# Attention probabilities turned by the DMA queue for three query tiles of four, with one ring of buffers for both kinds

## The chip, the cores and the metric

The kernel runs on one core of one Trainium2 chip. The time is device time in microseconds (us) from launch to end. Before the change it is 1529.46 us, the median of three runs (1526.32 to 1533.48).

The engines are named as the profile names them: PE is TensorE (PEld its weight loads), DVE VectorE, ACT ScalarE, POOL GpSimd, SP SyncE, whose queue issues most of the DMAs. Each engine works through its own instructions in order and waits at the first whose semaphores are not there yet.

## The reference, cut to what matters

Four sequences of 1024 tokens with 256 features run through four layers, each added to its input: a linear recurrence, a gated feed-forward layer, attention, and the feed-forward layer again. The change lies in the attention, which is, for each of 8 heads of 64:

```python
scores = jnp.einsum('bqhd,bkhd->bhqk', q, k) * scale      # 1024 x 1024 per head
attn = jax.nn.softmax(scores, axis=-1)
out = jnp.einsum('bhqk,bkhd->bqhd', attn, v)
```

The feed-forward layer that runs beside it picks, per token, the 32 largest of 256 gates (`top_k`) and multiplies with them.

## The kernel before, in words

There are three parts. The first, about 0 to 300 us, is the recurrence. The last, from about 1335 us, is the second feed-forward layer. Between them the attention runs, from about 378 to 1303 us, with the first feed-forward layer's remaining tiles (`f1.tile`, 24 tiles of 128 tokens) and the preparation of later work filled in beside it.

The attention's work is cut into **units**: a batch b (4), a half nb of its queries (2), a pair of heads g (4), and a tile q of 128 queries (4), so 128 units. The generator `heads` (L856) makes them one after another. A unit has two **steps**, one for each head j of the pair, so there are 256 steps. A step is:

- scores: four PE matmuls of 128 queries by 512 keys into `sc` (L886; keys are held in a high and a low part). `sc` has two buffers in PSUM.
- the row's maximum on DVE (L890), from PSUM.
- the exponential on ACT (L894), which also gives the row's sum; the result `pr` has three buffers.
- the transpose of `pr`, since the following product needs keys on the partitions. There are two ways.

The **PE way** (q odd, 64 units): eight PE transposes of 128x128 float32 (L905) into PSUM, and two ACT copies of 128x512 out of it into `p0`/`p1` (L910; in the last batch one of the two is done by DVE, L908).

The **DMA way** (q even, 64 units): the exponential is shifted by 2 to the 11th (one more small DVE instruction, L892), ACT casts `pr` to float16 (L897), POOL subtracts that from `pr` to get the remainder in float16 (L898), both halves stand in `pd` (128x2048, two buffers), and SP issues one DMA transpose of it into `d0` or `d1` (L899; two buffers each).

Then `values_sum` (L920) multiplies the transposed probabilities with the values and divides by the row sums. A unit of the PE way takes 16 float32 matmuls (the profile counts each float32 pass, 32 in all). A unit of the DMA way takes 48 float16 matmuls (high and low probabilities with high values, and high probabilities with low values; L930). Both need: the reciprocal of the row sums on DVE (L924), its spreading to 128 columns `rows` on POOL (L926), a PE transpose of that (L938), an ACT copy `rb` (L940) and a DVE product (L941).

When a unit is summed is set by two lists. A unit of the PE way is put on `pending` and summed in the first step of the next unit. A unit of the DMA way is put on `late` and summed in the second step of the next unit of the DMA way, which is two units later. At the end of each batch both lists are emptied at once (L917).

Around it, `merge` (L963) takes one step of `heads` and then those steps of the side work whose time, counted in steps, has come (L1187 to L1213). What each engine does first is then decided by a scheduler with a model of the instructions' durations; it fixes one order for each engine before the kernel runs.

The side work uses the same engines. For the text that follows these lines matter: the gate tiles' top-k on DVE (L674) in `wk`, with POOL's L613, L628, L656, L658 and L659 and DVE's L636; the output product's split on ACT and POOL (L952, L953); and the layer norms, whose short DVE instructions are L55 to L66.

Of the kernel before, what the change touches and what calls it, by code (L numbers as in the profile page):

```python
# [10 lines left out]
F32 = mybir.dt.float32  # L11
# [3 lines left out]
F16 = mybir.dt.float16  # L15
# [6 lines left out]
P = 128  # L22
B = 4
T = 1024
D = 256
KD = D // P
TPB = T // P
# [4 lines left out]
PAIRS = HEADS // 2  # L32
# [147 lines left out]
class Banks:  # L180


    def __init__(self, pool, bufs):
        self.pool, self.bufs = pool, bufs

    def tile(self, shape, tag, name):
        return self.pool.tile(shape, F32, tag=tag, name=name, bufs=self.bufs[tag])
# [300 lines left out]
class Ffn:  # L488
# [100 lines left out]
    def tile(self, i, sp, psum, tags, out=None, fast=False, parts=None, tt=None, fine=False):  # L589


        nc, w = self.nc, self.w
        pool = nc.vector if fast else nc.gpsimd
        x = self.x[i]
        blk, tk = i // 4, slice((i % 4) * P, (i % 4 + 1) * P)
        full = None
        if blk in self.full:
            full = sp.tile([P, D], F32, tag="full", name="full")
            nc.sync.dma_start(full, self.full[blk][:, i % 4, :])
        pl = psum.tile([P, 2, D], tags[0], "pl")  # L600
        self.logits_product(pl, i)


        nr = TOPK // 8
        m8 = sp.tile([P, 2, nr, 8], F32, tag="m8", name="m8")
        e8 = sp.tile([P, 2, 8], F32, tag="e8", name="e8")
        nm = sp.tile([P, 2], F32, tag="nm", name="nm")
        ssum = sp.tile([P, 2], F32, tag="ssum", name="ssum")
        ex = sp.tile([P, 2, D], F32, tag="ex", name="ex")
        wk = sp.tile([P, 2, D], F32, tag="wk", name="wk")  # L610
        for s in range(2):
            self.ordered(nc.vector.max, m8[:, s, 0, :], pl[:, s, :])
        nc.gpsimd.tensor_scalar(nm, m8[:, :, 0, 0], -1.0, 0.0, ALU.mult, ALU.add)  # L613
        for s in range(2):
            nc.scalar.activation(  # L615
                ex[:, s, :], pl[:, s, :], AF.Exp, bias=nm[:, s : s + 1], accum_out=ssum[:, s : s + 1]
            )
            self.last_exp = nc.scalar.activation(e8[:, s, :], m8[:, s, 0, :], AF.Exp, bias=nm[:, s : s + 1]).ins
        yield
        for r in range(nr):  # L620
            for s in range(2 if r else 0):
                self.ordered(nc.vector.max, m8[:, s, r, :], wk[:, s, :])
            for s in range(2):
                v, k = (wk, m8[:, s, r, :]) if r else (ex, e8[:, s, :])
                self.ordered(nc.vector.match_replace, wk[:, s, :], k, v[:, s, :], 0.0)
            if fine and r < nr - 1:
                yield
        pool.tensor_tensor(ex, ex, wk, ALU.subtract)  # L628
        rs = sp.tile([P, 2], F32, tag="rs", name="rs")
        nc.vector.reciprocal(rs, ssum)  # L630
        yield

        q = i % 4
        norm = self.norm[blk]
        if full is not None:
            nc.vector.scalar_tensor_tensor(full, full, rs[:, 0:1], ex[:, 0, :], ALU.mult, ALU.mult)  # L636
            ob = full
        else:
            if tt is not None:
                pf = psum.tile([P, D], tags[2], "pf")  # L640
                self.full_product(pf, tt, q)
            else:
                xn = sp.tile([P, D], F32, tag="fxn", name="fxn")
                with self.tc.issue_after(self.convolved):
                    nc.scalar.activation(
                        xn, x, AF.Identity, bias=norm[:, 1, q : q + 1], scale=norm[:, 0, q : q + 1]
                    )
                pf = self.product(sp, psum, tags, xn, None, parts)
            ob = sp.tile([P, D], F32, tag="ob", name="ob")
            nc.scalar.mul(ob, pf, rs[:, 0:1])  # L650
            pool.tensor_tensor(ob, ob, ex[:, 0, :], ALU.mult)  # L651
        yield

        xg = sp.tile([P, D], F32, tag="xg", name="xg", bufs=2)
        sc = sp.tile([P, 2], F32, tag="sc", name="sc")
        pool.tensor_scalar(sc, norm[:, :, q], rs[:, 1:2], 0.0, ALU.mult, ALU.add)  # L656
        nc.scalar.activation(xg, x, AF.Identity, bias=sc[:, 1:2], scale=sc[:, 0:1])
        pool.tensor_tensor(xg, xg, ex[:, 1, :], ALU.mult)  # L658
        nc.gpsimd.tensor_tensor(x, x, ob, ALU.add)  # L659
        pi = self.product(sp, psum, tags, xg, w.bias, parts)  # L660
        if out is None or fast:
            nc.vector.tensor_tensor(x, x, pi, ALU.add)
        else:
            yi = sp.tile([P, D], F32, tag="yi", name="yi")
            nc.scalar.copy(yi, pi)
            nc.gpsimd.tensor_tensor(x, x, yi, ALU.add)
        if out is not None:
            nc.sync.dma_start(out[i // 4][:, i % 4, :], x)
        yield
# [103 lines left out]
class Attention:  # L773
    def __init__(self, tc, x, ident, ident64, wqk, wvo, wd, sp, wp):
        self.nc, self.x, self.ident, self.ident64 = tc.nc, x, ident, ident64
        self.wqk, self.wvo, self.wd, self.sp, self.wp = wqk, wvo, wd, sp, wp
        self.hp = None
        self.k, self.xnt, self.qs, self.on = {}, {}, {}, {}

        self.sident = wp.tile([HD, HD], F32R, tag="sident", name="sident")  # L780
# [75 lines left out]
    def heads(self, b, psum):  # L856
# [2 lines left out]

        nc, sp, wp = self.nc, self.sp, self.hp  # L860
        kh, kl, la, lb = self.k[b]
        late, pending = [], []
        for nb, g, q in (
            (nb, g, q)
            for nb in range(2)
            for g in range(PAIRS)
            for q in ((0, 2, 1, 3) if b == B - 1 and nb and g == PAIRS - 1 else range(4))
        ):
            by_dma = q % 2 == 0
            if g == 0:  # L870
                self.on[b, nb, q] = wp.tile([P, PAIRS, P], F32, tag=f"on{q}", name=f"on{q}")
            qs = self.qs[b, nb, g]
            ssum = sp.tile([P, 2], F32, tag="ssum", name="ssum", bufs=4)
            if by_dma:
                pts = [wp.tile([P, 2 * TPB, P], F16, tag=f"d{j}", name=f"d{j}", bufs=2) for j in range(2)]
                parts = ((0, lb[0]), (TPB, lb[0]), (0, lb[1]))
                terms = [(v[:, c, :], i + c) for c in range(TPB) for i, v in parts]
            else:
                pts = [wp.tile([P, TPB, P], F32, tag=f"p{j}", name=f"p{j}") for j in range(2)]
                terms = [(la[:, c, :], c) for c in range(TPB)]  # L880
            for j in range(2):
                sc = psum.tile([P, T], "sc", "sc")
# [10 lines left out]
                pr = wp.tile([P, T], F32, tag="pr", name="pr", bufs=3)  # L893
                nc.scalar.activation(pr, sc, AF.Exp, bias=nm, accum_out=ssum[:, j : j + 1])  # L894
                if by_dma:
                    pd = wp.tile([P, 2, T], F16, tag="pd", name="pd", bufs=2)
                    nc.scalar.copy(pd[:, 0, :], pr)  # L897
                    nc.gpsimd.tensor_tensor(pd[:, 1, :], pr, pd[:, 0, :], ALU.subtract)  # L898
                    nc.sync.dma_start_transpose(pts[j], pd.rearrange("p i k -> p (i k)"))  # L899
                else:  # L900
                    for half in range(2):
                        pt = psum.tile([P, 4, P], "t", "ptp")
                        for kk in range(4):
                            kc = 4 * half + kk
                            nc.tensor.transpose(pt[:, kk, :], pr[:, kc * P : (kc + 1) * P], self.ident)  # L905
                        dst = pts[j][:, 4 * half : 4 * half + 4, :]
                        if half == 0 and b == B - 1:
                            nc.vector.tensor_copy(dst, pt)  # L908
                        else:
                            nc.scalar.copy(dst, pt)  # L910
                if j == 0 and pending:
                    self.values_sum(*pending.pop(0), psum)
                if j == 1 and late and by_dma != (q > 0 and (b, nb, g) == (B - 1, 1, PAIRS - 1)):
                    self.values_sum(*late.pop(0), psum)
                yield
            (late if by_dma else pending).append((pts, terms, ssum, self.on[b, nb, q][:, g, :]))
        for args in late + pending:  # L917
            self.values_sum(*args, psum)

    def values_sum(self, pts, terms, ssum, on, psum):  # L920

        nc, sp = self.nc, self.sp
        rs = sp.tile([P, 2], F32, tag="rs", name="rs")
        nc.vector.reciprocal(rs, ssum)  # L924
        rows = sp.tile([P, 2, HD], F32, tag="rows", name="rows")
        nc.gpsimd.tensor_copy(rows, rs[:, :, None].to_broadcast([P, 2, HD]))  # L926
        po = psum.tile([P, 2, P], "s", "pmo")
        for n, (v, c) in enumerate(terms):
            for j in range(2):
# [395 lines left out]
```

## Time and profile before

| what | before |
|---|---|
| median of three runs | 1529.46 us |
| the profiled execution: its time, its span | 1528.76 us, 1527.0 us |
| PE, DVE, ACT, POOL busy over the span | 84%, 78%, 67%, 45% |
| attention part (378 to 1303 us): PE, DVE, ACT, POOL busy | 831, 692, 706, 430 us of 925 us |
| granted TensorE clock, mean | 0.946 |
| DMA transposes | 128, of 128 x 2048 float16 each |
| DMA engines' mean busy share in the attention part | 0.39 to 0.45 |

A group of instructions in the profile stands as: line, engine, operation, output<-input with shapes, count, then busy time in us and the mean duration of one in ns, then the idle time of that engine just before it, and what ended most of that idle time. A wait stands as: engine and line that waited, who ended it, the total in us, how often, the longest.

### The profile page before, as it was taken

To read this page: it belongs to the slowest core of one execution; us is meant where nothing else is said; L and a number is where in the kernel's file an instruction comes from. 1 tells how busy PE (TensorE), PEld (TensorE's weight loads), DVE (VectorE), ACT (ScalarE), POOL (GpSimd) and SP (SyncE) were. 2 spreads that over 40 slices of the span, in tenths; PEclk is the share of its full clock that TensorE was granted. 3 is DMA by queue.
4 is the path that set the end of the run, shared out by engine and by line. 5 is a ranking of instruction groups with operands and counts; after the bars stand their busy time and mean duration, and the time that the engine had idled before them with its cause. 6 is when DMAs were issued, how large, how long until landed. Compare 5 with 4: busy or idle time off the path is not lost. (4 is left out here: it accounts for less than half of the span.)

```text
span 1527.0 us, 28727 instructions
## 1 busy us (share of the span) xinstructions
PE 1286.5 (84%) x10134; PEld 955.6 (63%) x10136; DVE 1184.6 (78%) x3682; ACT 1017.5 (67%) x2152; POOL 680.3 (45%) x849
## 2 busy tenths in 40 slices
PE   4879998697898898888998989889999999566675
PEld 3535465376677766766776767677777777334454
DVE  8976665697868887878768687777676675599998
ACT  5353433566887877797777787877777776475674
POOL 2033332161545454544544554454344444067776
PEclk9999999698999999999999999999999999688899
DMA  3110000321454343434433445334344545000000
GB/s 118 32 41 15 21 21 21 128 97 49 84 93 90 61 77 73 77 70 82 82 74 60 72 79 86 61 61 83 68 82 79 92 86 96 1 15 24 22 25 28
DMA packets 288609, 96.51 MB, mean 63 GB/s; under 512 B 268233, under 2 KB 284626, under 8 KB 288466
## 3 DMA queue, kind: packets, MB, share of 16 engines
q1 hardware_dynamic: 283024, 88.50, 28.7%
q10 hardware_dynamic: 5442, 6.18, 1.2%
q8 instruction: 80, 1.31, 0.4%
q14 instruction: 63, 0.52, 0.1%
HBM read 16.01 MB, written 11.53 MB: 18 GB/s over the span
## 5 line engine op out<-in xcount | busy, mean ns | idle before, releaser
L898 POOL TENSOR_TENSOR pd<-pr,pd 128x1024 f16<-128x1024 f32 x128 | 273.5, 2141 | 247.6 <-ACT pd L897 185.7
L890 DVE TENSOR_REDUCE nm<-sc 128x1 f32<-128x1024 f32 x256 | 308.5, 1217 | 78.9 <-PE sc L886 77.5
L894 ACT ACTIVATE pr<-sc,nm 128x1024 f32<-128x1024 f32 x256 | 285.9, 1119 | 84.6 <-DVE nm L892 47.0
L886 PE MATMUL sc<-kh,qs 128*128 128x512 f32 x512 | 184.3, 438 | 26.4 <-ACT pr L894 18.8
L886 PE MATMUL sc<-kl,qs 128*128 128x512 f32 x512 | 162.0, 397 | 0.0
L674 DVE MATCH_REPLACE8 wk<-m,wk 128x256 f32<-128x256 f32 x384 | 154.9, 406 | 0.1
L910 ACT COPY p<-ptp 128x512 f32<-128x512 f32 x224 | 124.1, 590 | 45.3 <-PE ptp L905 33.7
L674 DVE MAX8 m<-wk 128x8 f32<-128x256 f32 x384 | 151.3, 412 | 0.4
L930 PE MATMUL pmo<-p,la 128*64 128x128 f32 x2048 | 144.0, 289 | 6.1 <-ACT ft L524 2.9
L905 PE MATMUL ptp<-ident,pr 128*128 128x128 f32 x1024 | 138.3, 275 | 12.9 <-ACT pr L894 12.4
L930 PEld LDWEIGHTS pmo<-p,la 128*64 128x64 f32 x2048 | 122.8, 144 | 25.0 <-ACT ft L524 5.1
L905 PEld LDWEIGHTS ptp<-ident,pr 128*128 128x128 f32 x1024 | 115.6, 140 | 34.8 <-ACT pr L894 22.2
L897 ACT CAST pd<-pr 128x1024 f16<-128x1024 f32 x128 | 133.5, 1054 | 5.6 <-DMA d<-pd 4.6
L886 PEld LDWEIGHTS sc<-kh,qs 128*128 128x128 f32 x512 | 85.2, 195 | 51.1 <-ACT pr L894 29.8
L886 PEld LDWEIGHTS sc<-kl,qs 128*128 128x128 f32 x512 | 97.0, 190 | 23.2 <-issue 1.4
L930 PE MATMUL pmo<-d,lb 128*64 128x128 f16 x3072 | 103.4, 222 | 7.6 <-DVE qs L853 2.6
L930 PEld LDWEIGHTS <-lb 128*64 128x64 f16 x3072 | 92.2, 111 | 26.3 <-issue 20.1
L628 POOL TENSOR_TENSOR ex<-ex,wk 128x512 f32<-128x512 f32 x61 | 77.6, 1273 | 57.4 <-DVE wk L674 45.5
L926 POOL COPY rows<-rs 128x128 f32<-128x128 f32 x128 | 36.1, 294 | 124.4 <-PE pmo L938 76.3
L941 DVE TENSOR_TENSOR on<-pmo,rb 128x128 f32<-128x128 f32 x128 | 36.4, 285 | 66.8 <-ACT rb L940 66.3
L147 PE MATMUL pt<-ident,xn 128*128 128x128 f32 x256 | 47.8, 309 | 44.5 <-ACT xn L145 32.9
L699 PE MATMUL pf<-wf,vt 128*128 128x256 f32 x288 | 81.2, 427 | 4.6 <-ACT vt L697 4.2
(307 smaller groups left out, 2768.6 us busy)
## 6 DMA issues: line engine op xcount, KB each, us to landing
tt<-ft SPq DMA_DIRECT2D x16, 256.0 KB
tt<-tt SPq DMA_DIRECT2D x8, 512.0 KB
out<-x SPq DMA_DIRECT2D x32, 128.0 KB
x<-in_x ACTq DMA_DIRECT2D x6, 512.0 KB
pf<-pfs SPq DMA_DIRECT2D x12, 256.0 KB
full<-pf SPq DMA_DIRECT2D x24, 128.0 KB
d<-pd SPq DMA_TRANSPOSE x128
wa<-in_w_attn SPq DMA_DIRECT2D x2, 640.0 KB
```

Of the source, the lines that this page charges most:

```text
L147: nc.tensor.transpose(pt[:, k, i * P : (i + 1) * P], xn[:, k * P : (k + 1) * P], ident)
L628: pool.tensor_tensor(ex, ex, wk, ALU.subtract)
L674: ins = make(*args).ins
L699: nc.tensor.matmul(dst, vt[:, k, :], w.wf[:, k, :], start=(k == 0 and bias is None), stop=(k == KD - 1))
L886: nc.tensor.matmul(sc[:, sl], qs[:, j, q * P : (q + 1) * P], kk[:, sl], start=(i == 0), stop=(i == 1))
L890: nc.vector.tensor_reduce(nm, sc, AX.X, ALU.max, negate=True)
L894: nc.scalar.activation(pr, sc, AF.Exp, bias=nm, accum_out=ssum[:, j : j + 1])
L897: nc.scalar.copy(pd[:, 0, :], pr)
L898: nc.gpsimd.tensor_tensor(pd[:, 1, :], pr, pd[:, 0, :], ALU.subtract)
L905: nc.tensor.transpose(pt[:, kk, :], pr[:, kc * P : (kc + 1) * P], self.ident)
L910: nc.scalar.copy(dst, pt)
L930: nc.tensor.matmul(po[j * HD : (j + 1) * HD, 0, :], v, pts[j][:, c, :], start=(n == 0), stop=(n == len(terms) - 1),)
```

## The change

Three of the four query tiles (q below 3) now go the DMA way, in place of two (q even). Only the last pair of heads of the last half of the last batch keeps the alternation. So 95 units go the DMA way in place of 64, and 33 the PE way.

The separate buffers `d0`/`d1` (two each) and `p0`/`p1` (one each) are replaced by one ring of three for each head, `p0`/`p1`; a unit of the DMA way sees its buffer as float16. `pd` gets three buffers in place of two. The row sums `ssum` get six in place of four. The top-k's `wk` gets one buffer in place of two in the tiles that run beside the attention.

The two lists become one, `due`, which is kept over the ends of the batches. In the first step of each unit the reciprocals (and `rows`) of the unit two back are made, and in the second step that unit is summed, whichever way it went. After the last unit what is left is summed at once.

```diff
-        wk = sp.tile([P, 2, D], F32, tag="wk", name="wk")
+        wk = sp.tile([P, 2, D], F32, tag="wk", name="wk", **({"bufs": 1} if fine else {}))
...
+        self.due = []
...
-        late, pending = [], []
...
-            by_dma = q % 2 == 0
+            by_dma = q % 2 == 0 if (b, nb, g) == (B - 1, 1, PAIRS - 1) else q < 3
...
-            ssum = sp.tile([P, 2], F32, tag="ssum", name="ssum", bufs=4)
+            ssum = sp.tile([P, 2], F32, tag="ssum", name="ssum", bufs=6)
+            pts = [wp.tile([P, TPB, P], F32, tag=f"p{j}", name=f"p{j}", bufs=3) for j in range(2)]
             if by_dma:
-                pts = [wp.tile([P, 2 * TPB, P], F16, tag=f"d{j}", name=f"d{j}", bufs=2) for j in range(2)]
+                pts = [t.bitcast(F16).rearrange("p c (i q) -> p (c i) q", i=2) for t in pts]
...
             else:
-                pts = [wp.tile([P, TPB, P], F32, tag=f"p{j}", name=f"p{j}") for j in range(2)]
                 terms = [(la[:, c, :], c) for c in range(TPB)]
...
-                    pd = wp.tile([P, 2, T], F16, tag="pd", name="pd", bufs=2)
+                    pd = wp.tile([P, 2, T], F16, tag="pd", name="pd", bufs=3)
...
-                if j == 0 and pending:
-                    self.values_sum(*pending.pop(0), psum)
-                if j == 1 and late and by_dma != (q > 0 and (b, nb, g) == (B - 1, 1, PAIRS - 1)):
-                    self.values_sum(*late.pop(0), psum)
+                if j == 0 and len(self.due) > 1:
+                    rows = self.reciprocals(self.due[0][2])
+                if j == 1 and len(self.due) > 1:
+                    self.values_sum(*self.due.pop(0), rows, psum)
                 yield
-            (late if by_dma else pending).append((pts, terms, ssum, self.on[b, nb, q][:, g, :]))
-        for args in late + pending:
-            self.values_sum(*args, psum)
-
-    def values_sum(self, pts, terms, ssum, on, psum):
+            self.due.append((pts, terms, ssum, self.on[b, nb, q][:, g, :]))
+        if b == B - 1:
+            for unit in self.due:
+                self.values_sum(*unit, self.reciprocals(unit[2]), psum)
+
+    def reciprocals(self, ssum):
 
         nc, sp = self.nc, self.sp
         rs = sp.tile([P, 2], F32, tag="rs", name="rs")
         nc.vector.reciprocal(rs, ssum)
         rows = sp.tile([P, 2, HD], F32, tag="rows", name="rows")
         nc.gpsimd.tensor_copy(rows, rs[:, :, None].to_broadcast([P, 2, HD]))
+        return rows
+
+    def values_sum(self, pts, terms, ssum, on, rows, psum):
```

More of the change, by code (lines that the diff above doesn't have):

```diff
@@ L926, in values_sum @@
         nc.gpsimd.tensor_copy(rows, rs[:, :, None].to_broadcast([P, 2, HD]))
+        return rows
+    def values_sum(self, pts, terms, ssum, on, rows, psum):
+        nc, sp = self.nc, self.sp
         po = psum.tile([P, 2, P], "s", "pmo")
```

## The prediction

> **What bounds the kernel now.** I read the busy times by stage first, since the change touches only the attention. These are the stages of its four batches. After the length, each pair is busy time and count of PE, PEld, DVE, ACT and POOL; then come the clock, the DMA share and GB/s:
>
> ```profile
> 378.00:606.00 228.00, 203.08 (x1993) 159.37 (x1992) 182.25 (x475) 180.43 (x363) 113.28 (x118) 0.99 0.44 80
> 606.00:853.00 247.00, 218.79 (x2143) 173.94 (x2142) 188.62 (x497) 187.78 (x374) 115.47 (x119) 0.97 0.39 74
> 853.00:1096.00 243.00, 215.76 (x2139) 172.06 (x2137) 182.19 (x471) 185.84 (x367) 111.13 (x111) 0.97 0.40 73
> 1096.00:1303.00 207.00, 193.80 (x2125) 157.63 (x2123) 138.93 (x283) 151.60 (x273) 90.17 (x77) 1.00 0.45 83
> ```
>
> PE is busy 89, 89, 89 and 94% of them, DVE 80 to 67%, ACT 79 to 73%, POOL 50 to 44%. Together: 925 us, PE 831, ACT 706, DVE 692, POOL 430. PE is the bound, but not alone: three engines at three quarters and more hand each step on in turn. The waits show it: PE waits for ACT's exponential, ACT for DVE's maximum, DVE for PE's scores.
>
> ```profile
> DVE nm L890 <- PE sc L886: 77.5, 78, 3.3
> ACT pr L894 <- DVE nm L892: 47.0, 34, 2.9
> PEld sc L886 <- ACT pr L894: 29.8, 32, 3.6
> DVE rs L924 <- ACT pr L894: 20.6, 20, 2.5
> ACT pd L897 <- DMA d<-pd: 4.6, 3, 2.2
> ```
>
> Last I read the groups of instructions for the two ways:
>
> ```profile
> L898 POOL TENSOR_TENSOR pd<-pr,pd 128x1024 f16<-128x1024 f32 x128 | 273.5, 2141 | 247.6 <-ACT pd L897 185.7
> L910 ACT COPY p<-ptp 128x512 f32<-128x512 f32 x224 | 124.1, 590 | 45.3 <-PE ptp L905 33.7
> L930 PE MATMUL pmo<-p,la 128*64 128x128 f32 x2048 | 144.0, 289 | 6.1 <-ACT ft L524 2.9
> L905 PE MATMUL ptp<-ident,pr 128*128 128x128 f32 x1024 | 138.3, 275 | 12.9 <-ACT pr L894 12.4
> L897 ACT CAST pd<-pr 128x1024 f16<-128x1024 f32 x128 | 133.5, 1054 | 5.6 <-DMA d<-pd 4.6
> L930 PE MATMUL pmo<-d,lb 128*64 128x128 f16 x3072 | 103.4, 222 | 7.6 <-DVE qs L853 2.6
> ```
>
> Matmuls overlap, so their busy time, not count times mean, is what they cost.
>
> **PE: what is taken away.** 31 units change ways (95 less 64). A PE-way unit costs 138.3/64 = 2.16 us of transposes and 144.0/64 = 2.25 us of sums; a DMA-way unit 103.4/64 = 1.62 us. That saves 2.79 us a unit, 87 us. From stretches of the chain of waits the terms are 2 x 1.02, 1.9 and 1.46 us, a saving of 2.5 us, 77 us. I take 83: PE falls from 831 to 748 us.
>
> **ACT: nothing.** Removed: 24 units x 4 copies and 7 units (last batch) x 2, 110 x 0.59 = 65 us. Added: 62 casts x 1.054 = 65 us.
>
> **DVE: a little.** Added: 62 small shifts (L892) at 0.143 us = 9 us. Removed: 14 copies (L908) at 0.684 us = 10 us. The reciprocals no longer wait for a row sum just being made: DVE loses the 20.6 us of waiting on ACT shown above, which is time ahead of the next maximum in its queue. I count it as cover for the next point, not as gain.
>
> **DVE against POOL.** POOL gets 62 x 2.141 = 133 us more, 563 in all. Nearly all its instructions read SBUF. The Trainium skill ("SBUF — State Buffer", section "SBUF: two separate sides") says that POOL and a DVE instruction with two SBUF inputs exclude one another for the whole instruction. The trace agrees: durations (min/median/max) of such a DVE instruction of 128x256, and of one of only 128x4:
>
> ```profile
> L636 DVE SCALAR_TENSOR_TENSOR full<-full,rs,ex x24: 474/864/2319, 402.1 to 1063.7; 128x256 f32<-128x256 f32 x24
> L64 DVE SCALAR_TENSOR_TENSOR ax_t<-ax_rs x18: 151/163/2125, 493.3 to 1075.2; 128x4 f32<-128x4 f32 x18
> ```
>
> The long ones have the length of a POOL subtraction. The excess of mean over the short case, for L636 24 x 0.50, for L55 to L66 about 21 us together, is 33 us now. It grows with POOL's share of the time, 430/925 = 0.46 to 563/880 = 0.64: plus 13 us. If every such instruction met a full subtraction (about 150 of them, 2.1 us) the rule would cost over 300 us; the short medians speak against that. If none met more than now, nothing. I take 13. The maximum L890 reads PSUM; L890's fixed 1.2 us shows no such spread. DVE ends at 692 + 9 - 10 + 13 = 704.
>
> **DMA.** 62 more transposes, 190 in all. By the skill's "VectorE: DVE Perf Modes", section "The three transpose paths", TensorE should be chosen where PSUM will do: 390 ns against 1309 ns for a 128x128 tile. By that rule a DMA-way unit (32 tiles) takes 42 us, 95 units nearly 4000 us, and this change would be a disaster. The trace's landings say otherwise: of two transposes issued one behind the other the second lands 2.26 us (median) after the first, so 16 tiles cost 0.14 us each. A group of four units needs 6 x 2.26 = 13.6 us of DMA in some 27 us. I use the trace: DMA throughput costs nothing. Latency: a transpose lands 4.4 us after its issue (median), and half the sums start over 12 us after their data is there, since the summing is two units behind. SP's queue also carries the 24 loads of `full`; they wait for a buffer that POOL's L659 frees and hold up the transposes behind them, as they do now (23 us of waiting in all, all under that slack).
>
> **The buffers.** From a cast's start to its landing are 8.0 us (median): 1.05 cast, 2.14 subtraction, 4.4 transfer, the rest waiting. With three `pd` buffers, ACT can cast once per 8.0/3 = 2.7 us; a step takes 925/256 = 3.6 us now. That is cover of 2.8 us per round of three, and it is gone when POOL has its other work in the way (L953 1.28, L628 1.28, L658 0.80, L659 0.73 us). ACT then stands at the cast, and behind it stand the exponential of the next step, the evacuations for PE and with them the scores. Low end: 0. High end: the 4.1 us of those four per group of four units, 32 groups, 131 us. The nearest row is the wait of three casts above, 4.6 us in all at two buffers but with every second unit free of casts. I take 10 us. The ring of three for `p0`/`p1`: unit i+3 writes about a step after unit i is summed, but its own scores, exponential, cast and subtraction (over 6 us) come first; nothing. `wk` with one buffer: the next tile's top-k begins 8 steps after the last one's and that lasts 4 or 5, so 3 steps cover it: nothing, unless POOL's L628 is over 10 us late. At the very end two units are left to sum in place of one: plus 2 us; the ends of the first three batches no longer flush their lists, minus about as much.
>
> **The sum.** Two ends. If PE keeps its share of 90%, the stage takes 748/0.9 = 832, minus 93 us. If instead the sum of the three engines' shares stays at (831+706+692)/925 = 2.41, since each waits for the others, it takes (748+706+704)/2.41 = 895, minus 30 us. Batch 0 shows that 2.48 is possible: 870, minus 55. I stay near that, minus 55, and put the 10 us of casts against it: minus 45. 1528.8 (the profiled execution: span 1527.0 and 1.8 around it; the runs' median is 1529.5, so they are one number here) - 45 = 1483 us. Its own range is 1462 to 1512. What is late next is the ring of scores, maximum and exponential, with ACT at 706/880 = 80% and PE at 85%.
>
> **Rivals.**
>
> *PE's saving comes through whole* (15%): the waits shrink with the work, minus 70 to minus 93: about 1448. For it: PE at 94% in the last batch, with ACT at 73%. Against it: ACT and DVE do not get less work and PE waits mostly for these.
>
> *No change* (11%): the exponential's chain sets the pace. By the waits, DVE and ACT wait over 70 us each on this chain; if those do not shrink and 15 us come to it, 1521 to 1537. Against it: ACT and DVE have 20 to 25% of slack.
>
> *Slower* (27%): POOL's queue and the `pd` buffers tie ACT to the DMA. In the changed order three units in a row need six subtractions, 12.8 us, plus POOL's other 4 to 6 us, in about 20 us; any delay goes through the `pd` buffer to ACT's cast. In the order of the changed program 10 of 190 casts stand two or three exponentials behind their own, in the old order none: the schedule already makes room for it, and by holding `pr`. It decides from a stall of (83 - 13)/32 = 2.2 us per group of four units on; at the 3.2 us that lie between that and the high end, 32 x 3.2 = 102 against 70, and with the full high end 131 against 70: 1561 to 1590, and from some 1540 when PE's saving is only partly felt. For it: POOL waits now because ACT is late, but its 2.14 us is the longest instruction of the step. Against it: POOL is at 64% on average, and the fourth unit needs nothing of it.
>
> **How the numbers follow.** About 0.5% (7.6 us) is what can be told from no change. The likely case has 47%, the full saving 15%: faster 0.62. No change 0.11, slower 0.27. The range is 1436 to 1548: it leaves out the worst of the slow case, some 14%, and little below.
>
> **What would show it.** PE in the attention stage near 748 us, with 33 x 16 transposes left; POOL near 563; ACT unchanged within 10; the attention from 925 to about 880. If ACT's cast waits for the DMA over 40 us in sum, or L898 delays `pr`, the slow rival is right. If DVE's L636 and L64 to L66 grow by far more than 13 us, my port term is too small. If PE's sums wait for landings, the two-unit lag was not enough. I am wrong at the root if PE's busy time falls by less than 70 us.

## The result, and the profile after

The changed kernel takes 1581.26 us, the median of four runs (1579.88 to 1584.27); the kernel before took 1529.02 us beside it (four runs). The ratio is 1.0344, with a 95% interval of 1.0318 to 1.037: 52 us slower, where 1483 us was forecast. The profiled execution has a span of 1579.6 us (1527.0 before) and a mean granted TensorE clock of 0.919 (0.946).

The loss lies in the attention alone. These are the stages of its four batches after the change, with the columns of the same view before: length, busy time and count of PE, PEld, DVE, ACT and POOL, clock, DMA share, GB/s.

```profile
376.70:630.90 254.20, 202.40 (x1937) 153.79 (x1937) 189.90 (x490) 179.12 (x344) 146.47 (x133) 0.89 0.59 103
630.90:887.30 256.40, 207.90 (x2141) 157.21 (x2140) 196.44 (x512) 187.56 (x358) 147.65 (x133) 0.95 0.60 105
887.30:1144.00 256.70, 207.40 (x2139) 158.89 (x2137) 186.22 (x486) 185.40 (x351) 145.11 (x128) 0.94 0.59 102
1144.00:1355.00 211.00, 185.75 (x2175) 147.56 (x2175) 136.25 (x284) 159.30 (x275) 121.30 (x93) 0.98 0.68 116
```

Against the rows before, the batches are 26, 9, 14 and 4 us longer. ACT and DVE have nearly the work they had, POOL a good 30 us more in each. PE, which was to gain, is busy nearly as long as before in batch 0 (202 for 203 us), at a clock of 0.89 in place of 0.99.

The waits of the attention: who waited for whom, the sum in us, how often, the longest.

```profile
PEld sc L886 <- ACT pr L894: 102.1, 82, 8.1
DVE nm L890 <- PE sc L886: 99.8, 88, 5.2
ACT pd L897 <- DMA p<-pd: 59.0, 43, 5.4
DVE rs L925 <- ACT pr L894: 55.2, 37, 3.4
ACT pr L894 <- DVE nm L892: 47.0, 41, 3.7
PE pmo L936 <- DMA p<-pd: 11.4, 12, 2.1
```

The waits of the ring of scores, maximum and exponential have grown or stayed, but for ACT's on the maximum itself (L890), which fell from 26.2 to 21.1 us. PE's wait for the exponential went from 29.8 to 102.1 us, DVE's for the scores from 77.5 to 99.8. ACT's cast waits 59.0 us for a transpose to land and free its `pd` buffer (4.6 before). The wait of the reciprocals, which I had counted as gone, went from 20.6 to 55.2 us.

The groups of the two ways:

```profile
L898 POOL TENSOR_TENSOR pd<-pr,pd 128x1024 f16<-128x1024 f32 x190 | 406.2, 2143 | 197.8 <-ACT pd L897 143.4
L897 ACT CAST pd<-pr 128x1024 f16<-128x1024 f32 x190 | 198.3, 1051 | 60.1 <-DMA p<-pd 59.0
L936 PE MATMUL pmo<-p,lb 128*64 128x128 f16 x4560 | 161.2, 224 | 26.5 <-DMA p<-pd 11.4
L905 PE MATMUL ptp<-ident,pr 128*128 128x128 f32 x528 | 78.3, 289 | 12.0 <-ACT pr L894 8.1
L936 PE MATMUL pmo<-p,la 128*64 128x128 f32 x1056 | 72.9, 295 | 11.9 <-DVE qs L854 8.2
L910 ACT COPY p<-ptp 128x512 f32<-128x512 f32 x114 | 63.5, 593 | 21.6 <-PE ptp L905 18.6
```

The counts are those the prediction reckoned with. The chain of work that ended last, traced back over the span, runs through transposes for about a tenth of it (the share named DMA). The same view of the kernel before follows its chain over 18% of the span only, so the two cannot be set against each other:

```profile
DVE 36%; PE 28%; ACT 13%; DMA 11%; issue 7%; POOL 4%; SPq 0%; ACTq 0%; POOLq 0%; DVEq 0%
```

One place shows how a transpose gets late. The first stretch is of POOL, the second of PE (start, length, instruction).

```profile
764.91 2.14 POOL L898 TENSOR_TENSOR pd<-pr,pd 128x1024 f16<-128x1024 f32 x1 [1.51 <-issue]
```

```profile
776.24 1.53 PE L936 MATMUL pmo<-p,lb 128*64 128x128 f16 x48
```

The subtraction that fills `pd` ends at 767.05. Its transpose is issued only at 777.8, when the last sum that reads the ring's oldest `p` buffer has ended (776.24 + 1.53). For those 10.7 us the `pd` buffer is held too, by a transpose that has not begun. Summed over the attention, the first head of each pair stood 311 us between the end of its subtraction and the issue of its transpose (77 before), the second 149 us (52 before). So the two rings of buffers are coupled, and behind `pd` stand ACT's cast and its next exponential.

### The profile page after: what moved, and what is told of

Its sections match the earlier page's. It is cut to its first block, busy times and chain, and to the rows that moved or that the text cites. A ratio compares the mean times of both kernels' runs of the same rounds, so it can differ in the third digit from the quotient of the medians.

```text
span 1579.6 us, 29096 instructions
## 1 busy us (share of the span) xinstructions
PE 1258.7 (80%) x10136; PEld 908.7 (58%) x10136; DVE 1200.6 (76%) x3730; ACT 1022.7 (65%) x2104; POOL 810.9 (51%) x911
## 4 chain that ended last, share of the span: by engine, by line
DVE 36%; PE 28%; ACT 13%; DMA 11%; issue 7%; POOL 4%; SPq 0%; ACTq 0%; POOLq 0%; DVEq 0%
DMA p<-pd 10%; DVE wk L674 8%; DVE nm L890 6%; DVE m L674 6%; PE pmo L936 5%; PE sc L886 5%; ACT pr L894 4%; PE po L437 2%; POOL pd L898 2%; ACT pd L897 2%; PE ptp L905 2%; PE pu L170 2%; PE pz L452 1%; DVE qs L854 1%; ACT p L910 1%
## 5 line engine op out<-in xcount | busy, mean ns | idle before, releaser
L898 POOL TENSOR_TENSOR pd<-pr,pd 128x1024 f16<-128x1024 f32 x190 | 406.2, 2143 | 197.8 <-ACT pd L897 143.4
L890 DVE TENSOR_REDUCE nm<-sc 128x1 f32<-128x1024 f32 x256 | 309.8, 1219 | 101.8 <-PE sc L886 99.8
L886 PE MATMUL sc<-kh,qs 128*128 128x512 f32 x512 | 191.2, 454 | 78.3 <-ACT pr L894 72.8
L897 ACT CAST pd<-pr 128x1024 f16<-128x1024 f32 x190 | 198.3, 1051 | 60.1 <-DMA p<-pd 59.0
L936 PE MATMUL pmo<-p,lb 128*64 128x128 f16 x4560 | 161.2, 224 | 26.5 <-DMA p<-pd 11.4
L936 PEld LDWEIGHTS <-lb 128*64 128x64 f16 x4560 | 140.7, 113 | 60.9 <-issue 52.7
L886 PE MATMUL sc<-kl,qs 128*128 128x512 f32 x512 | 169.4, 412 | 0.0
L886 PEld LDWEIGHTS sc<-kh,qs 128*128 128x128 f32 x512 | 89.8, 206 | 119.9 <-ACT pr L894 102.1
L886 PEld LDWEIGHTS sc<-kl,qs 128*128 128x128 f32 x512 | 101.1, 199 | 23.2
L927 POOL COPY rows<-rs 128x128 f32<-128x128 f32 x128 | 37.6, 294 | 107.1 <-PE pmo L944 75.9
L905 PE MATMUL ptp<-ident,pr 128*128 128x128 f32 x528 | 78.3, 289 | 12.0 <-ACT pr L894 8.1
L936 PE MATMUL pmo<-p,la 128*64 128x128 f32 x1056 | 72.9, 295 | 11.9 <-DVE qs L854 8.2
L556 PE MATMUL pl<-lint,xc_f 128*128 128x512 f32 x128 | 72.5, 654 | 9.6 <-ACT xc_f L587 9.6
L615 ACT ACTIVATE ex<-pl,nm 128x256 f32<-128x256 f32 x128 | 60.6, 475 | 28.6 <-POOL nm L613 27.9
L910 ACT COPY p<-ptp 128x512 f32<-128x512 f32 x114 | 63.5, 593 | 21.6 <-PE ptp L905 18.6
L936 PEld LDWEIGHTS pmo<-p,la 128*64 128x64 f32 x1056 | 64.3, 149 | 22.3 <-issue 11.1
```

The lines of the kernel that those rows point to most:

```text
L556: self.last_logits = nc.tensor.matmul(v, x, w.lint, start=False, stop=True).ins
L886: nc.tensor.matmul(sc[:, sl], qs[:, j, q * P : (q + 1) * P], kk[:, sl], start=(i == 0), stop=(i == 1))
L890: nc.vector.tensor_reduce(nm, sc, AX.X, ALU.max, negate=True)
L936: nc.tensor.matmul(po[j * HD : (j + 1) * HD, 0, :], v, pts[j][:, c, :], start=(n == 0), stop=(n == len(terms) - 1),)
```

## Experiments

Two theories stood at the start. **A**: the ring of three for `p` is held too long by the later sums. **B**: POOL and the `pd` buffers tie ACT to the DMA (the prediction's slow rival). When neither alone gave the time back, a third was added: PE's saved work was worth nothing to begin with. Each edit's diff is against the changed kernel unless it says before; every variant also gets its own fixed order from the scheduler. "Ring wait" is the sum of the stretches just described, first plus second heads: 129 us before, 460 after. The number after "casts" is ACT's wait for the DMA.

### Two of four again, in the new buffers

```diff
-            by_dma = q % 2 == 0 if (b, nb, g) == (B - 1, 1, PAIRS - 1) else q < 3
+            by_dma = q % 2 == 0
```

> The changed kernel with the two ways alternating again (q even by DMA), so with the work of the kernel before, but its one ring of three buffers, its three pd buffers and its summing at the second next unit. Theory A (the ring: a transpose waits on SP's queue until the unit three back is summed, the pd buffer is held meanwhile, and ACT stands at the cast): the ring turns over per unit as before, so part of the loss stays, 1540 to 1565 us, and the wait from a subtraction's end to its transpose's issue stays above 2 us a transpose in the mean for a unit's first head. Theory B (POOL's 133 us of subtractions in bursts of six): the bursts are gone, 1520 to 1535 us.

Measured: 1554.83 us, ratio 1.0159 (1.014 to 1.0177). The way of the units is the same as before, and 24 us are lost: by the shared ring, the later sums of the PE-way units, the early reciprocals, or the lists that are no longer emptied at each batch's end. Ring wait 488, casts 18.3 us. The other half of the loss comes with the third DMA-way unit.

### The sum one step earlier

```diff
-                    rows = self.reciprocals(self.due[0][2])
-                if j == 1 and len(self.due) > 1:
-                    self.values_sum(*self.due.pop(0), rows, psum)
+                    self.values_sum(*self.due[0], self.reciprocals(self.due[0][2]), psum)
+                    self.due.pop(0)
```

> The changed kernel with the reciprocals and the sum of the unit two back both in the first step, so each unit is summed one step (3.8 us) earlier and its ring buffer comes free earlier. Theory A: the waits of 311 us (subtraction's end to issue, first heads) fall to under 150 us and the time falls to 1535 to 1560 us. Theory B: POOL's bursts are the same, within 8 us of 1581.

Measured: 1595.8 us, 1.0435 (1.0418 to 1.0453). The ring wait fell to 310 and the casts to 35.6 us, as meant, yet the kernel got slower: ACT's exponential now waits 77.9 us for L892 (47.0). Shorter waits on the ring did not give time; this speaks against A alone.

### Room for buffers, a ring of four, two `pd`

Two kernels. The first only makes room: `ex`, `full` and `xg` of the tiles beside the attention get one buffer. The second adds the last two lines:

```diff
+            full = sp.tile([P, D], F32, tag="full", name="full", **({"bufs": 1} if fine else {}))
...
+        ex = sp.tile([P, 2, D], F32, tag="ex", name="ex", **({"bufs": 1} if fine else {}))
...
+        xg = sp.tile([P, D], F32, tag="xg", name="xg", bufs=1 if fine else 2)
...
+            pts = [wp.tile([P, TPB, P], F32, tag=f"p{j}", name=f"p{j}", bufs=4) for j in range(2)]
...
+                    pd = wp.tile([P, 2, T], F16, tag="pd", name="pd", bufs=2)
```

> The changed kernel with one buffer in place of two for ex, full and xg of the gate tiles beside the attention, to have memory for the next runs; their comparison. Both theories: 1578 to 1595 us.

> As e3, with a ring of four p buffers for each head and only two pd buffers in place of three. Theory A: transposes no longer wait for sums, faster than e3 by 30 to 70 us in spite of the smaller pd (1515 to 1555 us). Theory B: the smaller pd ties ACT more tightly to POOL and the DMA, slower than e3 by 20 us or more.

Measured: 1582.16 us, 1.0341 (1.0322 to 1.036), so the room costs nothing; and 1623.2 us, 1.0615 (1.0585 to 1.0646). The waits of the second in the attention:

```profile
POOL pd L898 <- ACT pd L897: 193.4, 98, 5.3
ACT pd L897 <- DMA p<-pd: 120.8, 85, 4.0
```

The ring wait is back at what it was before the change (129 us), but the cast's wait doubles (59.8 in the first of the two), and 41 us are lost with one `pd` buffer less, for all the fourth `p`. B is real, and it is the stronger of the two at that point.

### More memory, then a ring of four or five `pd`

The first kernel makes more room: the gate tiles' product is made in plain float32, without the split weights `wfs`, besides the small buffers of the control above. The other two add to it `p` with four buffers, or `pd` with five (the last two lines, one in each):

```diff
-        wfs = two([P, KD, D], "wf")
-        nc.scalar.copy(wfs[0], w.wf)
-        nc.gpsimd.tensor_tensor(wfs[1], w.wf, wfs[0].bitcast(F32), ALU.subtract)
...
-            side.append((start, f1.tile(i, fp, psum, "sss", parts=wfs, fine=True), [1, 1, 1, 1, 1, 2, 1]))
+            side.append((start, f1.tile(i, fp, psum, "sss", fine=True), [1, 1, 1, 1, 1, 2, 1]))
...
+            pts = [wp.tile([P, TPB, P], F32, tag=f"p{j}", name=f"p{j}", bufs=4) for j in range(2)]
...
+                    pd = wp.tile([P, 2, T], F16, tag="pd", name="pd", bufs=5)
```

> As e3, and the gate tiles' product beside the attention in plain float32 from the weights as they are (two fewer 2 KB weight tiles, no DVE split), to have memory for the next two runs; their comparison. 1570 to 1600 us by every theory.

> As e5 with a ring of four p buffers and the three pd buffers kept. Theory A (the ring): transposes stop waiting for sums, ACT's wait for pd falls under 25 us, faster than e5 by 30 to 60 us. Theory B (the time from cast to landing against the number of pd buffers, with POOL's bursts in it): the p ring matters little, within 12 us of e5. Both tie (each holds the other's buffers): 12 to 30 us faster.

> As e5 with five pd buffers and the ring of three kept. Theory A: subtracted data wait in pd for the ring, ACT passes on for two casts more, a small gain, 5 to 20 us faster than e5, and the transposes still wait over 250 us for sums. Theory B: ACT's wait for pd falls from about 59 us to under 10 us and the time falls by 40 us or more.

Measured: 1572.23 us (1.026; 1.0237 to 1.0283), 1572.31 us (1.0266; 1.0244 to 1.0289) and 1554.5 us (1.0148; 1.0119 to 1.0177). The control is itself 10 us faster than the one above. The ring of four takes the ring wait from 571 to 217 us and gains nothing. Its casts still wait:

```profile
ACT pd L897 <- DMA p<-pd: 38.1, 30, 2.9
```

Five `pd` buffers leave the ring wait long (742 us), take the casts' wait from 67.4 us in the control to 0.5, and gain 18 us. A as the sole cause falls with the ring of four. B's wait went as expected, but it was worth 18 us and not the 40 or more that B asked for; a small gain with the ring waits left is what A had expected of this kernel.

### Alternation with the reciprocals made late

```diff
+            by_dma = q % 2 == 0
...
-                if j == 0 and len(self.due) > 1:
-                    rows = self.reciprocals(self.due[0][2])
...
-                    self.values_sum(*self.due.pop(0), rows, psum)
+                    unit = self.due.pop(0)
+                    self.values_sum(*unit, self.reciprocals(unit[2]), psum)
```

> As e1 (the two ways alternating, ring of three), with the reciprocals made together with the sum in the second step and not a step ahead. If the early reciprocals are what e1 lost 24 us by (DVE waits 36 us for row sums and 29 us for rows there, before 21 and 0), this gives 1528 to 1542 us; if the ring and the later sum of the PE-way units are, it stays at 1548 to 1560 us.

Measured: 1555.62 us, 1.0158 (1.0143 to 1.0173), the same as the first experiment: the early reciprocals cost no time.

### Less PE work in the kernel before

Against before. The DMA way's sum keeps one of its three products (two products with the smaller parts are left out): two thirds of 103.4 us, 69 us of PE work less, with no buffer and no other engine's work touched.

```diff
-                parts = ((0, lb[0]), (TPB, lb[0]), (0, lb[1]))
+                parts = ((0, lb[0]),)
```

> The kernel before, with the sums of the DMA-way units cut from 48 to 16 matmuls: the products with the low halves of the probabilities and of the values are left out. That takes 64 x 1.08 = 69 us of work from PE and nothing from any other engine, nor a buffer. If PE is the bound as the prediction had it: 45 to 70 us faster than before (1460 to 1485). Theory D (PE's busy time was never what the stage ran at; ACT, DVE and the order fixed ahead are): within 15 us of before.

Measured: 1532.34 us (20 runs), 1.0023 (1.0011 to 1.0036). The profiled execution is the slowest of the twenty (1541.91 us), and its attention runs to 1316 us; with the columns of the stages above:

```profile
378.00:1316.10 938.10, 802.65 (x6349) 629.30 (x6348) 699.61 (x1725) 704.32 (x1378) 429.46 (x422) 0.95 0.42 76
```

and two waits of the ring of scores (77.5 and 29.8 us before):

```profile
DVE nm L890 <- PE sc L886: 124.4, 94, 6.8
PEld sc L886 <- ACT pr L894: 41.5, 37, 3.6
```

PE's saved work bought no time. The group that was cut went from 103.4 to 44.5 us, 59 less. PE's busy time fell by 28 only (831 to 803), because the matmuls that stayed took some 30 us more: those of the scores went from 346 to 363 us, while the clock was 0.95 over the stage in place of 0.98. What was left of the saving turned into waits. The stage of this execution is 13 us longer than before; 10 of these are what it lies above the median of its kernel. It is sums that were taken away here and not transposes, but this one number takes away the gain that the prediction rested on.

### Alternation with a ring of four

The alternation of the first experiment, the small side buffers, `p` with four buffers, `pd` with two as in the kernel before.

```diff
+            by_dma = q % 2 == 0
...
+            pts = [wp.tile([P, TPB, P], F32, tag=f"p{j}", name=f"p{j}", bufs=4) for j in range(2)]
...
+                    pd = wp.tile([P, 2, T], F16, tag="pd", name="pd", bufs=2)
```

> As e1 with a ring of four p buffers and two pd buffers as the kernel before has (the small side buffers of e3 pay for it). If e1's 24 us are the ring of three, whose transposes wait 277 + 211 us for sums there, this gives 1525 to 1540 us and those waits fall below 150 us; if they are the later sum of the PE-way units or the order, 1548 us or more.

Measured: 1558.83 us, 1.0196 (1.0167 to 1.0225). Ring wait 186 in place of 488 us, no gain, although ACT's cast waits no longer with one `pd` buffer less (17.7 us, 18.3 there): the 24 us of the first experiment are not the ring's waits either.

### No gate tiles beside the attention

The first kernel is the one before without its 24 gate tiles and `wfs`. The second is the changed one without them, with `p` four and `pd` five buffers.

```diff
-        for i in range(TPB, NT):
-            n = i - TPB
-            start = 1 + 6.75 * n if n < TPB else STEPS * (n // TPB) - STEPS + 48.25 + 8 * (n % TPB + 1)
-            side.append((start, f1.tile(i, fp, psum, "sss", parts=wfs, fine=True), [1, 1, 1, 1, 1, 2, 1]))
```

> The kernel before without the 24 gate tiles beside the attention (their part of the first feed-forward layer is left out); the comparison for e12. Their PE work is under 100 us and they load DVE with about 190 us: 1400 to 1470 us.

> The changed kernel without those 24 gate tiles, with a ring of four and five pd buffers. If buffers alone stood in the way of PE's saving: faster than e11 by 40 to 80 us. Theory D: within 15 us of e11, since nothing that ACT or DVE does is less.

Measured: 1440.44 us (0.9419; 0.9394 to 0.9444) and 1471.43 us (0.9623; 0.9596 to 0.9649). The attention of the first:

```profile
378.00:1215.00 837.00, 782.91 (x8132) 634.00 (x8130) 503.10 (x1010) 655.51 (x1192) 354.32 (x302) 0.98 0.48 82
```

PE has 48 us less than before, DVE 189, ACT 50, POOL 76, and the stage ends some 90 us earlier. Where 69 us of PE alone gave nothing, this mix gives much; PE is then busy 94%. The changed kernel is 31 us behind even here, neither ahead nor level as the two expectations had it. Its ring wait is 34 us, and its casts do not wait, but the sums now do:

```profile
PE pmo L936 <- DMA p<-pd: 40.7, 36, 3.5
PEld L936 <- DMA p<-pd: 16.6, 17, 1.9
```

In this faster stage two units of distance are too little for the sums: the median one starts 0.2 us before its second transpose lands (7.6 us after it in the changed kernel).

### One buffer for `wk`, and the later sum, in the kernel before

Against before. The first kernel only gives `wk` one buffer (the first line). The second takes the units of the PE way in the second step of the second next unit, with room made by the small side buffers, six `ssum` and `p` with two buffers of its own:

```diff
+        wk = sp.tile([P, 2, D], F32, tag="wk", name="wk", **({"bufs": 1} if fine else {}))
...
+                pts = [wp.tile([P, TPB, P], F32, tag=f"p{j}", name=f"p{j}", bufs=2) for j in range(2)]
...
-                if j == 0 and pending:
+                if j == 1 and pending and not by_dma:
```

> The kernel before with one part of the change alone: one wk buffer for the gate tiles beside the attention. By the prediction (the next tile's top-k begins three steps after the last one's end) it costs nothing, 1525 to 1534 us. If it is what e1 and e10 lost 24 to 28 us by: 1545 us or more.

> The kernel before with another part alone: units of the PE way are summed in the second step of the second next unit, as the change does, in place of the first step of the next (two p buffers for it, the small side buffers of e3 and e13's wk pay for them). If the later sum is what e1 lost by: e13 plus 15 to 25 us. If not: within 6 us of e13.

Measured: 1528.87 us, 1.0 (0.9988 to 1.0012); and 1539.19 us, 1.0064 (1.004 to 1.0088). `wk` costs nothing. Summing the PE-way units later costs about 10 us with separate rings, which lies between the two expectations.

### Half the subtraction

In the changed kernel `pd` becomes three fixed buffers, and POOL subtracts over half the keys (the remainders of the other 512 keys are left out, as zeros).

```diff
-                    nc.gpsimd.tensor_tensor(pd[:, 1, :], pr, pd[:, 0, :], ALU.subtract)
+                    nc.gpsimd.tensor_tensor(pd[:, 1, 0:512], pr[:, 0:512], pd[:, 0, 0:512], ALU.subtract)
```

> The changed kernel with POOL's subtraction over half the keys (the low halves of the other 512 keys' probabilities are left out and stay zero; three fixed pd buffers). It takes 190 x 1.07 = 203 us from POOL. Theory B (POOL's bursts make cast to landing long): ACT's wait for pd falls under 20 us and the time to 1550 us or less, as with five pd buffers (e7: 18 us faster than its comparison). If POOL matters little: within 8 us of 1581.

Measured: 1556.9 us, 1.0177 (1.0148 to 1.0207), 24 us of the 52 back. POOL's work is part of the price, but not in the way expected. ACT's wait for `pd` was to fall under 20 us and is as long as in the changed kernel (59.0), and the ring wait rose from 460 to 596 us:

```profile
ACT pd L903 <- DMA p<-pd: 62.2, 36, 4.3
```

```profile
376.00:1326.80 950.80, 796.02 (x8396) 608.57 (x8394) 678.11 (x1773) 711.59 (x1330) 376.54 (x484) 0.96 0.63 109
```

What fell besides POOL's work (561 to 377 us) is DVE's, from 709 to 678 us for the same instructions. Nearly all of the 31 us lie in those that the prediction's port term was about, L636 and the short ones of the layer norms; the 18 of L64 into `ax_t` took 7.4 us in place of 16.2. So the gain may have come through DVE and not through `pd`. No kernel here separates the two.

### The PE-way units summed early again

Once in the changed kernel, once with the alternation of the first experiment:

```diff
+                if j == 0 and self.due and self.due[-1][0] is None:
+                    unit = self.due.pop()[1]
+                    self.values_sum(*unit, self.reciprocals(unit[2]), psum)
+                if j == 1 and self.due and self.due[0][0] <= at - 2:
+                    unit = self.due.pop(0)[1]
+                    self.values_sum(*unit, self.reciprocals(unit[2]), psum)
```

> The changed kernel with PE-way units summed in the first step of the next unit as before, and DMA-way units still at the second next. If the later sum of PE-way units costs (e14): 12 to 25 us faster than the changed kernel, 1556 to 1569 us. If not: within 8 us of 1581.

> As e8 (the two ways alternating, ring of three, reciprocals with the sum), with the PE-way units summed in the first step of the next unit again. Nothing but the shared ring, wk (e13: no cost), pd with three buffers and the missing flush then tells it from the kernel before. If the later sum was e1's loss: 1527 to 1540 us. If not, 1548 us or more, and the shared ring or the order is left.

Measured: 1583.78 us, 1.0348 (1.0314 to 1.0382), and 1534.66 us, 1.0032 (1.0019 to 1.0045). With the alternation 20 of the 24 us come back; in the changed kernel nothing does, although ring wait (220 us) and casts (41.8 us) both fell. One wait tells the two apart: POOL's copy `rows`, which stands in POOL's queue with the subtractions, waiting for PE to have read the earlier `rows`. It is 76 us before. In the alternating kernels with the later sum it is 130 to 149 us (four of four), and with the early sum:

```profile
POOL rows L930 <- PE pmo L947: 73.2, 38, 6.1
```

In the changed kernel it is 75.9 us, and 74.8 with the early sum. That fits all six, but not the rest: the control with more memory has 62.3 us of it and its ring of four 111.4, at the same time, and the last kernel below has 125.7 and is the fastest of those with three DMA-way units that keep the gate tiles. No kernel changed this wait alone, so that it costs time is not shown.

### All reliefs at once

The control with more memory, with `p` four buffers, three fixed `pd` buffers and half the subtraction:

```diff
+            pts = [wp.tile([P, TPB, P], F32, tag=f"p{j}", name=f"p{j}", bufs=4) for j in range(2)]
...
+                    nc.gpsimd.tensor_tensor(pd[:, 1, 0:512], pr[:, 0:512], pd[:, 0, 0:512], ALU.subtract)
```

> The comparison of e5 with everything relieved that was suspected and fits: a ring of four, three fixed pd buffers, and POOL's subtraction over half the keys as in e15 (those low halves left out). If buffers and POOL are all that is lost, PE's saved work should leave it at or below the kernel before: 1520 to 1535 us. If what is left after e7 and e15 (about 25 us) belongs to the order of work and its longer way from scores to sums: 1542 us or more.

Measured: 1529.28 us (12 runs), 1.0006 (0.9991 to 1.002): 43 us below its control, equal to before. Its attention up to 1303 us (it ends 2 us later), and three waits of it (its lines stand a few numbers lower in the file, L887 for L886 and so on):

```profile
378.00:1303.00 925.00, 786.79 (x8328) 606.08 (x8328) 668.13 (x1747) 705.45 (x1328) 376.89 (x484) 0.95 0.64 112
```

```profile
PEld sc L887 <- ACT pr L895: 67.6, 71, 4.8
ACT pr L895 <- DVE nm L893: 70.5, 52, 4.0
ACT pd L903 <- DMA p<-pd: 15.6, 16, 2.9
```

Against this control the ring of four alone gained nothing, and against the changed kernel half the subtraction alone gained 24 us; both together take away 43, the whole loss of the control. And with the loss gone nothing of a gain appears: PE has 44 us less than before in the stage and waits 37.8 us longer for the exponential. Even to come level this kernel had help that has nothing to do with PE: 24 us less on DVE and 53 us less on POOL than before, from the half subtraction and the product that is not split. No kernel here beat the one before by more than can be told from no change, those without gate tiles apart.

## Why the prediction was wrong

**The step that failed is the first: "PE is the bound, but not alone", and with it "The sum. Two ends."** Both ends, -93 and -30 us, gave PE's saved work a price, and I took 55 us for 83. The runs show a price of nothing: 69 us less PE work by counts in the kernel before gave 1.0023, and the changed kernel with its buffers and half of POOL's subtraction relieved came to 1.0006. Of the 97 us between the forecast (-45) and the result (+52), 55 are this term. A busy share of 89% was read as a bound. The lines that spoke against it were in the same view: PE waited for ACT, ACT for DVE, DVE for PE. What the stage follows more nearly is DVE's and ACT's work, as the kernels without tiles and the half subtraction (DVE 31 us less, the time 24) suggest; which link of that ring sets the pace was not isolated. The rival "no change" named this mechanism, and I gave it 11%.

**PE's own term** was 831 to 748 us; it measured 804 (the whole 978.9 us of the attention), so the line "wrong at the root if PE's busy time falls by less than 70" applies. The removed work was right to within 14 us: transposes from 138.3 to 78.3, sums from 247.4 to 234.1 us (161.2 + 72.9), 73 in all against 87 by counts. But a group's busy time is not what it costs, as the prediction had it, for the groups overlap each other too: theirs add up to 1007 us in the attention before, where PE is busy 834 (from 376 us on). And the same 1024 matmuls of the scores went from 346 to 361 us (191.2 + 169.4 after), and most other groups grew a little, while the clock fell from 0.98 to 0.94 over the stage. The Trainium skill ("TensorE: Matmul & The Clock Gate", section "What's actually happening") says that the clock is released by activity and held back by default. The trace agrees in direction: batch 0 has 89% busy PE at 0.99 before and 80% at 0.89 after. The share alone does not give the clock: the next two batches after, with 81%, stand at 0.95 and 0.94. The prediction kept the old clock for a PE with less to do.

**The `pd` buffers** were costed at 10 us between 0 and 131. ACT's wait was 59.0 us in 43 casts, and taking it away gains 18 us (five buffers): the mechanism was right and its size too small. I measured cast to landing at 8.0 us and divided by three; the median rose to 9.3 us and the mean from 9.1 to 10.9, because the transposes wait for `p`. The figure was taken from a state that the change itself ended. **POOL's added work** was priced only through these buffers and as 13 us of DVE. Halving the subtraction gave 24 us while the wait for `pd` stayed, so POOL costs time in another way as well, perhaps through DVE; whether that term was missing or only too small is open.

**The ring of three for `p`, "nothing"**, was wrong: 460 us of ring wait in place of 129. I counted when the next unit would write, and not that in SP's queue a transpose which waits for `p` holds a filled `pd`. Its price is not separate: alone, four in place of three gives 0.

**The later sum of the PE-way units** was not costed at all. It is 10 us with separate rings and 20 in the shared one with alternation. With three of four going the DMA way it shows no price of its own.

**The reciprocals' wait** was to vanish and grew to 55.2 us; why was not isolated. Made late or early in the alternating kernel, the time is the same (1555.62 and 1554.83 us), so there this error cost nothing.

**Right**: ACT's work (711 us, forecast 706), DVE's (709, forecast 704), POOL's (561, forecast 563), the DMA's throughput, and `wk` with one buffer. The port term was of the right order as DVE time: in the attention L636 stayed, while the short ones grew, here with their minimum, median and maximum:

```profile
L636 DVE SCALAR_TENSOR_TENSOR full<-full,rs,ex x24: 476/612/2451, 399.3 to 1107.6; 128x256 f32<-128x256 f32 x24
L64 DVE SCALAR_TENSOR_TENSOR ax_t<-ax_rs x18: 136/163/2070, 495.8 to 1121.2; 128x4 f32<-128x4 f32 x18
```

L64's mean went from 615 to 899 ns with the median where it was: more of them were long. The groups concerned took some 20 us more, forecast 13.

**The slow rival** (27%, 1561 to 1590) named the time and the `pd` mechanism, and its mark, a cast wait over 40 us, was met. Its sum was wrong twice over: it set 102 to 131 us of stalls against 70 us of PE's gain. With the 59 us measured it would itself have said 1518 (1528.8 - 70 + 59). There was less stall, and no gain to set it against.

**Still open**: how the 52 us divide between `p`, `pd` and POOL, which hold one another's buffers (a fourth `p` alone 0, five `pd` 18, half the subtraction 24, the first and the last together 43); whether the subtraction costs through the buffers or through DVE's longer instructions; what the third DMA-way unit changes so that the early sum no longer helps; and how much of each difference is the fixed order, which is new in every kernel. Half the subtraction in the kernel before was not tried.

## What to carry to other kernels

Before an engine's saved work is given a price, take a similar amount away from the kernel before and time it: one experiment would have shown zero here, for an engine that was 89% busy. Buffers that hand on to one another (here `pd` to the transpose to `p` to the sum) are one chain: the holding time of each has to be worked out with the next one late, and a relief of one link can show nothing until the next is relieved. A profile's waits can shrink without the time following, as in the second experiment, so a wait is a suspect and not yet a cost.

## What was not expected of the hardware

Taking matmuls away made the others slower: with 69 us less PE work by counts in the kernel before, the mean clock over the attention was 0.95 in place of 0.98, and over the run 0.918 to 0.928 in its twenty executions, against 0.936 to 0.949 in those of the kernel before beside them. The group that was cut lost 59 us, and some 30 of these came back as longer durations of the other matmuls. And the DMA engines took 190 transposes for 128 at a mean share of 0.6 in place of 0.4 without being the limit: with ample buffers no cast waited for them, and only the sums' distance became too short.
